# Layer 0 of a graph network: the transposed pattern made by TensorE, or from packed bytes by DMA, with the in-degrees on their own

## The chip, the cores and the metric

The kernel is one program on one core of a Trainium2 chip. The metric is the time of one execution on the device in microseconds, lower is better; times are medians of several executions. The core has a matrix engine (TensorE, PE in the profile), a vector engine (VectorE, DVE), a scalar engine (ScalarE, ACT), a general engine (GpSimd, POOL) and a sync engine (SyncE, SP). Each takes its own instructions in order; SP, ACT and POOL also issue DMA transfers.

## The reference

`x` is 2708 x 512 in float32, `adj` a symmetric 2708 x 2708 int32 matrix of zeros and ones. Four layers of a graph network run one after another, each on a normalized input, each adding its output to `x`:

```
h = relu(layernorm(x));  a = adj as float
# layer 0
x = x + relu((a.T @ h @ weight) * clip(a.sum(axis=0), 1) ** -0.5)
# layer 1: the first 64 neighbours of each row
h = relu(layernorm(x))
keep = (adj > 0) & (cumsum(adj > 0, axis=1) <= 64);  cnt = keep.sum(axis=1)
x = x + leaky(h @ W_line.T + b_line) + where(cnt > 0, leaky((keep @ h) / max(cnt, 1) @ W_nb.T + b_nb), 0)
# layer 2: attention over the neighbours, 8 heads of 64
# layer 3
h = relu(layernorm(x))
agg = (adj > 0) @ h / max(adj.sum(axis=1), 1)
x = x + relu(concat(h @ W_self + b_self, agg @ W_nb + b_nb) @ W_comb + b_comb)
```

Layer 0 multiplies with `adj` transposed, so a row block of `adj` serves as it lies, with its rows as the contracted axis. Layers 1 to 3 contract over columns and need each block of `adj` transposed.

## The kernel before

Rows are cut into `NC` = 22 chunks of `R` = 126; the last has 62 rows. `twice` and `TAIL` treat that last chunk by laying its rows down twice, at partition 0 and at 64.

**Dense parts.** Every layer has one. `staged` emits a pipeline: at step s, each stage works on chunk s minus its lag, in the order `load` (lag 0, `load_x` on SP), `normalize` (1, `norm` on VectorE with one square root on ScalarE: `ln_st` L191, `ln_mv` L193, `ln_rs`, `hn` L205), `transpose` (2, `relu_T`: `hT_ps` L214 on TensorE, evicted by ScalarE as `hT` L216) and `multiply` (3, the product). The product's result is split by `halves` into a rounded float32 and its remainder (L256, L258), two fp32r parts that later matmuls sum. There are `XBUFS` = 5 buffers for x tiles.

**Layer 0** is one long `staged` pipeline over units (g, m): six groups g of output chunks (4, 4, 4, 4, 3, 3) and, in each, all 22 row blocks m. The dense part of layer 0 is woven into group 0. A unit goes through:

- `load0`, lag 0: SP loads `ai`, the int32 block of 126 rows and up to 506 columns (5 buffers).
- `count0`, lag 4: VectorE casts it to fp32r (`ar` L450, 3 buffers), ScalarE squares it to bf16 (`ab` L452, 3 buffers), VectorE scans it (`cum` L458, 2 buffers): the running count of neighbours along the row, continued over groups through `deg` (L466).
- `sign0`, lag 5: ScalarE compares the running count with 64 (L473) and sums the signs, from which the last kept column of every row follows.
- `save0`, lag 6: stores finished rows of the residual. `multiply0`, lag 6: TensorE multiplies the block's 2 x 4 products into four accumulators (`acc` L348, through `matmuls`), then transposes the block by four matmuls with `ab` as weights and an identity (`vT_ps` L501). The identity has a column of ones, so each result carries the block's column sums too. VectorE copies these sums (L504), ScalarE evicts the transposed block as int8 into `vT` (L513), which stays in on-chip memory for layers 1 to 3.

At the last row block of a group the in-degrees are summed and turned into `nrm` (L508 to L511), the accumulators are evicted by VectorE (L531) and ScalarE (L535) by turns, and the residual x is added (L537, by GpSimd; by VectorE in the last group). `x` of a group is loaded at its middle.

The Tile framework keeps an order of instructions on each engine close to the order of emission, by its own estimates; buffers come free when their last reader is done.

**The turn to layer 1.** Three steps of layer 1's dense part are emitted within layer 0's last group, at the row blocks `AHEAD` = (9, 13, 18). The remaining ones follow: `product1` multiplies with two weights (`nb_ps`, `line_ps`, both through `product` L186), adds a bias and the leaky relu (L604, L605), and adds that to x on GpSimd (L608). `spread_last` lays the last kept columns along rows as `lastr` (L588, L594). Then layer 1's `aggregate` starts, whose weights `kt` (L623) combine `lastr` and `vT`; `vT` is read by the attention (L762) and by layer 3 (L1170) as well. In the tables below, the attention's small matmuls are at L945.

## Time and profile before

| | us |
|---|---|
| median of 3 executions | 1849.98 (1847.86 to 1853.67) |
| the profiled execution, its own time | 1852.72 |
| its span | 1850.8 |
| TensorE busy in it | 1805.7 (98%) |
| VectorE, ScalarE, GpSimd busy | 1323.8, 843.7, 211.8 |
| mean granted TensorE clock | 0.995 |

The profile is of one execution. A row of a group of instructions gives the line, engine and operation, the output and inputs with their shapes, the count, the busy time and the mean time of one in ns, then the idle time of the engine ahead of it and what ended that idle. A row of waits gives the engine and line that waited, what it waited for, the total in us, the number of times and the longest. A timeline row gives start and duration in us, and joins equal instructions (x8). Matmul durations in it overlap: the time that matters is from start to start. Layer 0 ends at about 402 us of the span, layer 1's dense part at 571.

### The profile page before, as it was taken

The numbers are of one execution on the slowest core, as the hardware profiler recorded it, in microseconds if no ns is written. First come the engines' busy times: TensorE is split into PE (matmuls) and PEld (weight loads), VectorE is DVE, ScalarE is ACT, GpSimd is POOL, SyncE is SP. The second block draws the span as 40 slices with busy tenths as digits, with TensorE's granted clock in tenths as the row PEclk, the third lists the DMA queues.
The fourth block names the chain that finished last, engine by engine and source line by source line (L and its number), as shares of the span: only waits on it lengthen the run. The fifth ranks groups of instructions, "written<-read, shape, count | busy, mean of one in ns | idle before, by whom it ended". The sixth has DMA issues, their size and how long they took to land.

```text
span 1850.8 us, 30734 instructions
## 1 busy us (share of the span) xinstructions
PE 1805.7 (98%) x11878; PEld 1050.0 (57%) x11878; DVE 1323.8 (72%) x1997; ACT 843.7 (46%) x1536; POOL 211.8 (11%) x190
## 2 busy tenths in 40 slices
PE   9999999889999999999999999999999999999998
PEld 4556667654446887754444344444344455478786
DVE  4755888874444566687889999999999777533334
ACT  2545887762220000056697776776743566500000
POOL 0001011211110112156100000000000222100000
PEclk9999999999999999999999999999999999999999
DMA  7323555542223112253330220121112444303221
GB/s 243 117 79 106 150 161 149 144 127 65 68 73 82 45 45 67 65 159 102 96 91 18 60 56 15 56 61 40 29 32 51 119 137 133 103 23 105 96 67 44
DMA packets 126027, 161.03 MB, mean 87 GB/s; under 512 B 57394, under 2 KB 77982, under 8 KB 124990
## 3 DMA queue, kind: packets, MB, share of 16 engines
q1 hardware_dynamic: 106812, 123.60, 23.1%
q10 hardware_dynamic: 18484, 33.28, 5.4%
q0 software_dynamic: 576, 2.10, 0.3%
q8 instruction: 95, 1.56, 0.3%
q14 instruction: 60, 0.49, 0.1%
HBM read 111.34 MB, written 47.42 MB: 86 GB/s over the span
## 4 chain that ended last, share of the span: by engine, by line
PE 61%; DVE 16%; issue 5%; DMA 4%; ACT 2%; POOL 0%; SPq 0%; DVEq 0%; ACTq 0%; POOLq 0%
PE acc L348 25%; PE av L945 10%; DVE t L762 9%; PE nb_ps L186 8%; PE sums L945 4%; PE wh_ps L186 4%; PE self_ps L186 4%; PE line_ps L186 4%; DVE cum L458 4%; DMA rb<-rT 2%; PE hT_ps L214 1%; DMA ai<-in_adj 1%; DMA x<-x 1%; DVE ar L450 1%; ACT cum L473 1%
## 5 line engine op out<-in xcount | busy, mean ns | idle before, releaser
L762 DVE SCALAR_TENSOR_TENSOR t<-rb,ec,vT 126x2708 f32<-126x2708 f32 (+2 forms) x220 | 532.6, 2471 | 21.5 <-PE sums L945 12.4
L348 PE MATMUL acc<-halves,kt 126*126 126x512 f32 x1848 | 434.8, 395 | 3.7 <-DVE kt L623 2.1
L945 PE MATMUL av<-t,whs 126*32 126x451 f32 (+3 forms) x4576 | 436.6, 515 | 1.3 <-ACT whs L751 0.8
L348 PEld LDWEIGHTS acc<-halves,kt 126*126 126x126 f32 x1848 | 342.6, 186 | 92.5 <-DVE kt L623 6.2
L945 PEld LDWEIGHTS av<-t,whs 126*32 126x32 f32 (+1 forms) x4576 | 161.9, 110 | 205.5 <-issue 180.1
L348 PE MATMUL acc<-halves,ar 126*126 126x512 f32 x924 | 253.2, 413 | 6.5 <-ACT vT L513 3.5
L780 ACT ACTIVATE b<-t,eb 126x2708 bf16<-126x2708 f32 (+1 forms) x78 | 199.0, 2552 | 21.6 <-DVE t L762 21.4
L348 PEld LDWEIGHTS acc<-halves,ar 126*126 126x126 f32 x924 | 163.8, 187 | 51.0 <-issue 9.2
L623 DVE SCALAR_TENSOR_TENSOR kt<-lastr,index,vT 126x504 fp32r<-126x504 int16 (+3 forms) x154 | 110.4, 728 | 81.7 <-PE acc L348 81.5
L195 ACT ACTIVATE ln_rs<-ln_mv,eps 126x1 f32<-126x1 f32 x88 | 25.6, 294 | 283.9 <-DMA x<-x 199.2
L1170 DVE CAST kt<-vT 126x504 fp32r<-126x504 int8 (+3 forms) x154 | 56.0, 366 | 137.8 <-PE acc L348 137.8
L458 DVE TENSOR_TENSOR_SCAN cum<-ai,deg 126x504 int16<-126x504 int32 (+2 forms) x110 | 126.0, 1156 | 32.9 <-DMA ai<-in_adj 21.5
L945 PE MATMUL sums<-t,whs 126*32 126x338 f32 (+5 forms) x1568 | 141.0, 451 | 5.6 <-ACT out L984 5.6
L751 ACT ACTIVATE whs<-wh,ef 126x64 f32<-126x64 f32 x220 | 76.3, 349 | 128.3 <-PE sums L945 73.1
L912 POOL TENSOR_SCALAR z<-y 126x512 f32<-126x512 f32 x22 | 44.0, 2001 | 666.9 <-DVE y L905 658.2
L473 ACT ACTIVATE cum<-cum,limit 126x504 int16<-126x504 int16 (+3 forms) x132 | 88.4, 670 | 62.1 <-DVE deg L466 60.0
L945 PEld LDWEIGHTS sums<-t,whs 126*32 126x32 f32 (+1 forms) x1568 | 56.0, 109 | 73.3 <-issue 39.1
L191 DVE BATCH_NORM_STATS2 ln_st<-x 126x6 f32<-126x512 f32 x88 | 60.4, 686 | 48.7 <-DMA x<-x 40.9
L513 ACT CAST vT<-vT_ps 126x504 int8<-126x504 f32 (+1 forms) x132 | 70.1, 536 | 29.2 <-DVE sums L504 20.0
L186 PE MATMUL nb_ps<-wfn,hT 128*126 128x512 f32 x176 | 81.2, 605 | 2.0 <-ACT hT L216 2.0
L186 PE MATMUL nb_ps<-wn,hT 128*126 128x512 f32 x176 | 81.4, 606 | 0.0
L186 PE MATMUL h_ps<-w0s,hT 128*126 128x512 f32 x176 | 79.9, 597 | 1.4 <-ACT hT L216 1.1
(178 smaller groups left out, 1972.7 us busy)
## 6 DMA issues: line engine op xcount, KB each, us to landing
x<-x SPq DMA_DIRECT2D x105, 252.0 KB
x<-x ACTq DMA_DIRECT2D x84, 252.0 KB
ai<-in_adj SPq DMA_DIRECT2D x84, 249.0 KB
x<-in_x SPq DMA_DIRECT2D x42, 252.0 KB
rb<-rT SPq DMA_DIRECT2D x7, 1332.8 KB
wh<-whd SPq DMA_DIRECT2D x70, 94.5 KB
whd<-wh SPq DMA_DIRECT2D x21, 252.0 KB
aT<-avT SPq DMA_DIRECT2D x21, 252.0 KB
```

What stands on the lines that cost most here:

```text
L186: nc.tensor.matmul(po[:n], lhsT[:, f, :n], w[:, f, :], start=(f == 0), stop=(f == NF - 1))
L191: nc.vector.bn_stats(st[:n], xc[:n])
L348: nc.tensor.matmul(acc[:R], weight[:, k * R : (k + 1) * R], parts[:, i, :], start=(m == 0 and i == 0), stop=(m == NC - 1),)
L458: nc.vector.tensor_tensor_scan(cum[:n, :gw], ai[:n, :gw], ai[:n, :gw], 0.0 if g == 0 else deg[:n, m : m + 1], op0=ALU.add, op1=ALU.max,)
L473: nc.scalar.activation(cum[:n, :gw], cum[:n, :gw], AF.Sign, bias=limit[:n], scale=-1.0, accum_out=signs[:n, m, g : g + 1],)
L513: nc.scalar.copy(vT[g][:, :, m * R : (m + 1) * R], pt[:R, :K, :R])
L623: nc.vector.scalar_tensor_tensor(by_chunk(kt, cs), lastr[:, cs[0] * R : (cs[-1] + 1) * R].rearrange("p (c r) -> p c r", r=R), index[:R, m ...
L751: nc.scalar.activation(t[:q, :O], wh.pop((u, m))[:q], AF.Copy, scale=by)
L762: ins = nc.vector.scalar_tensor_tensor(t[:q, : hi - lo], row[h][:q, lo:hi], ec[:q, m, h : h + 1], vT[g][:q, k, lo:hi], op0=ALU.max, op1=AL ...
L780: nc.scalar.activation(b[:q, : hi - lo], weight[s][:q, : hi - lo], AF.Sigmoid, bias=eb[:q, m, h : h + 1], scale=STEEP,)
L945: nc.tensor.matmul(p[j * S : (j + 1) * S, : b - a], lhsT, rhs[:, part * size + a : part * size + b], start=(s % NC == 0), stop=(s % NC == ...
L1170: nc.vector.tensor_copy(by_chunk(kt, cs), pattern(m, cs))
```

## The change

The transposed pattern is no longer made by TensorE within layer 0. Rows of `adj` and of layer 0's x are taken in pairs: of each 252 rows, the even ones form one block and the odd ones the next (`paired`). For every two blocks VectorE packs the two 0/1 values into one int16, 256 times the odd one plus the even one (`two`), and GpSimd stores it to DRAM (`packed`, 66 stores). In layer 1's dense part, each of 22 steps fetches one chunk's columns from there with two transposing DMAs issued by SP: a large one into `vT` (2-byte elements, 128 x 1264) and a small one (128 x 128) for the last rows, of which VectorE copies the part needed (`turn` at lag 4, `finish` at lag 6; the line numbers of the changed kernel are L692, L698 for the DMAs and L704 for the copy). A transposing DMA is ordered behind the load of x four chunks on. `vT` now takes the memory that layer 0's buffers leave.

The fp32r block `ar` is made by ScalarE's square, whose sum goes into a check at the end (`squares`); the bf16 block and VectorE's cast are gone. The in-degrees come from matmuls of their own: 32 columns of ones times the upper halves of `ar`, four chunks side by side in four column groups, emitted for four row blocks at a time into one accumulator; ScalarE copies that at the last but two row blocks, TensorE transposes it at the last.

`ai` has 10 buffers, `ar` 10, `cum` 5. `count0` and `sign0` of later units are ordered behind the last group's norm, evictions and copy (`fenced`), and `save0` and `multiply0` have lag 7. In the last group one residual lies in the tag "t", so that it takes no buffer of x. The row counts go to DRAM and back to be put into natural order (`degd`, `rdeg`; used at L660), ahead of x loads on SP. `lastr` is written in natural order (L675, L685).

```diff
-    ident1 = const.tile([P, P], BF16, name="ident1")
-    nc.gpsimd.memset(ident1, 1.0)
-    nc.vector.tensor_copy(ident1[:, :R], ident[:, :R])
+    oneb = const.tile([P, 32], BF16, name="oneb")
+    nc.gpsimd.memset(oneb, 1.0)
...
+    def paired(src, c):
+        if c >= NC - 2:
+            return natural(src, c)
+        first = c // 2 * 2 * R
+        return src[first : first + 2 * R, :].rearrange("(r e) d -> e r d", e=2)[c % 2]
...
-    vpool = ctx.enter_context(tc.tile_pool(name="vpool", bufs=1, side="right"))
-    vT = [vpool.tile([R, len(cs), NC * R], I8, name=f"vT{g}") for g, cs in enumerate(groups)]
+    VW = -(-NC * R // 32) * 32
+    PAIRS = -(-(NC - 2) * R // 32) * 16
+    assert NC % 2 == 0
+    vT = []
+    packed = [
+        dram.tile([NC * R // 2, len(cs) * R + P - R], I16, name=f"packed{g}")
+        for g, cs in enumerate(groups)
+    ]
+    degd = dram.tile([NC, R], F32, name="degd")
...
+                (4, lambda c: turn(c)),
+                (6, lambda c: finish(c)),
...
+                ai = wk.tile([R, WG + P - R], I32, name="ai", bufs=10)
+                block = paired(adj, m)[:, c0 : c0 + wide]
...
+            def fenced(stage):
+                def fn(i):
+                    with ExitStack() as behind:
+                        for ins in fences.values():
+                            behind.enter_context(tc.issue_after(ins))
+                        stage(i)
+                return fn
...
-                ar = wk.tile([R, WG], F32R, name="ar", bufs=3)
-                nc.vector.tensor_copy(ar[:, :gw], ai[:, :gw])
-                ab = wk.tile([R, WG + P - R], BF16, name="ab", bufs=3)
-                nc.scalar.activation(ab[:n, :wide], ai[:n, :wide], AF.Square)
-                if wide < KR + P - R:
-                    nc.gpsimd.memset(ab[:n, wide : KR + P - R], 0.0)
+                ar = wk.tile([R, WG], F32R, name="ar", bufs=10)
+                nc.scalar.activation(
+                    ar[:, :gw], ai[:, :gw], AF.Square, accum_out=squares[:R, m, g : g + 1]
+                )
                 if gw < KR:
                     nc.vector.memset(ar[:, gw:KR].bitcast(F32), 0.0)
-                cum = wk.tile([R, WG], I16, name="cum", bufs=2)
+                cum = wk.tile([R, WG], I16, name="cum", bufs=5)
...
+                if m % 2 == 0:
+                    two = wk.tile([R, WG + P - R], I16, name="two", bufs=3)
+                    nc.vector.scalar_tensor_tensor(
+                        two[:, :wide],
+                        tiles[i + 1][0][:, :wide],
+                        256.0,
+                        ai[:, :wide],
+                        op0=ALU.mult,
+                        op1=ALU.add,
+                    )
+                    if wide < KR + P - R:
+                        nc.gpsimd.memset(two[:, wide : KR + P - R], 0)
...
+                if two is not None:
+                    to = packed[g][m // 2 * R : (m // 2 + 1) * R, :]
+                    nc.gpsimd.dma_start(to, two[:, : to.shape[1]])
...
-                def products():
-                    for k, c in enumerate(cs):
-                        matmuls(acc[c], h0[m], ar, k, m)
-                if m < NC - 1:
-                    products()
-                pt = ps.tile([P, KMAX, P], F32, name="vT_ps", tag="ps")
-                for k in range(K):
-                    nc.tensor.matmul(
-                        pt[:, k, :], ab[:n, k * R : k * R + P], ident1[:n], start=True, stop=True
+                uppers[m] = ar.bitcast(BF16)
+                batch = range(0)
+                if m == NC - 3:
+                    for j in (1, 2):
+                        uppers[m + j] = tiles[i + j][0].bitcast(BF16)
+                    batch = range(m // 4 * 4, NC)
+                elif m % 4 == 3:
+                    batch = range(m - 3, m + 1)
+                if m == 3:
+                    sums[g] = ps.tile([P, 2 * P], F32, name="sums_ps", tag="ps")
+                for j in batch:
+                    q = rows(j)
+                    for k in range(K):
+                        nc.tensor.matmul(
+                            sums[g][k * 32 : (k + 1) * 32, :R],
+                            oneb[:q],
+                            uppers[j][:q, 2 * k * R + 1 : 2 * (k + 1) * R : 2],
+                            start=(j == 0),
+                            stop=(j == NC - 1),
+                        )
+                if m == NC - 3:
+                    by_col = sums[g, 0] = common.tile([P, D], F32, name="by_col", tag="t", bufs=3)[:, :R]
+                    ins = nc.scalar.copy(by_col[: K * 32], sums[g][: K * 32, :R])
+                    fences["act"] = ins.ins
+                for k, c in enumerate(cs):
+                    matmuls(acc[c], h0[m], ar, k, m)
+                if m == NC - 1:
+                    pt = sums.pop(g)[:R, P:]
+                    nc.tensor.transpose(
+                        pt[:, : K * 32], sums.pop((g, 0))[: K * 32], ident[: K * 32, : K * 32]
                     )
-                nc.vector.tensor_copy(sums[g][:, :K, m : m + 1], pt[:R, :K, R : R + 1])
-                if m == NC - 1:
-                    nrm = small.tile([R, KMAX], F32, name="nrm")
-                    total = ind[:R, cs[0] : cs[-1] + 1]
-                    nc.vector.tensor_reduce(total, sums[g][:, :K], AX.X, ALU.add)
-                    nc.vector.tensor_scalar(nrm[:, :K], total, 1.0, None, op0=ALU.max)
+                    nrm = sums[g, 1] = small.tile([R, KMAX, 1], F32, name="nrm")
+                    nc.vector.tensor_scalar(
+                        nrm[:, :K],
+                        pt[:, : K * 32].rearrange("p (k j) -> p k j", j=32)[:, :, :1],
+                        1.0,
+                        None,
+                        op0=ALU.max,
+                    )
                     nc.scalar.activation(nrm[:, :K], nrm[:, :K], AF.Sqrt)
-                    nc.vector.reciprocal(nrm[:, :K], nrm[:, :K])
-                    products()
-                nc.scalar.copy(vT[g][:, :, m * R : (m + 1) * R], pt[:R, :K, :R])
+                    ins = nc.vector.reciprocal(nrm[:, :K], nrm[:, :K])
+                    fences["dve"] = ins.ins
...
+                    for k, c in enumerate(cs):
+                        tag, bufs = ("t", 3) if g == len(groups) - 1 and k == 0 else ("x", XBUFS)
+                        xs[c] = load_x(x_in, c, tag=tag, bufs=bufs)
...
+                        fences["dve"] = ins.ins
                     else:
-                        nc.scalar.activation(r[:n], po[:n], AF.Relu, scale=nrm[:n, k : k + 1])
+                        ins = nc.scalar.activation(r[:n], po[:n], AF.Relu, scale=nrm[:n, k])
+                        fences["act"] = ins.ins
...
+                (4, fenced(count0)),
+                (5, fenced(sign0)),
+                (7, save0),
+                (7, multiply0),
...
+        vpool = ctx.enter_context(tc.tile_pool(name="vpool", bufs=1))
+        vT.extend(
+            vpool.tile([P, len(cs), VW], mybir.dt.uint8, name=f"vT{g}")
+            for g, cs in enumerate(groups)
+        )
...
+        even = NC - 2
+        nc.sync.dma_start(
+            degd[:even].rearrange("(b f) r -> b (f r)", f=2).rearrange("b (r e) -> r b e", e=2),
+            deg[:R, :even].rearrange("r (b e) -> r b e", e=2),
+        )
+        nc.sync.dma_start(degd[even:].rearrange("c r -> r c"), deg[:R, even:])
         rdeg = const.tile([P, NC], F32, name="rdeg")
-        nc.vector.tensor_scalar(rdeg, deg, 1.0, None, op0=ALU.max)
+        nc.gpsimd.memset(rdeg, 1.0)
+        nc.sync.dma_start(rdeg[:R], degd.rearrange("c r -> r c"))
+        rcnt = const.tile([P, NC], F32, name="rcnt")
+        nc.vector.tensor_scalar(rcnt, rdeg, float(NEIGHBORS), 1.0, op0=ALU.min, op1=ALU.max)
...
+        def turn(c):
+            g, k = where[c]
+            own = slice(k * R, k * R + P)
+            with tc.issue_after(loads[min(c + 4, NC - 1)]):
+                nc.sync.dma_start(
+                    vT[g][:, k, : 2 * PAIRS].bitcast(I16), packed[g][:PAIRS, own], transpose=True
+                )
+            ends = wk.tile([P, P], I16, name="ends", bufs=4)
+            with tc.issue_after(loads[min(c + 4, NC - 1)]):
+                nc.sync.dma_start(ends, packed[g][NC * R // 2 - P :, own], transpose=True)
+            turned[c] = ends
+        def finish(c):
+            g, k = where[c]
+            ends = turned.pop(c)
+            nc.vector.tensor_copy(
+                vT[g][:, k, (NC - 2) * R : NC * R].rearrange("p (e r) -> p e r", e=2),
+                ends[:, P - R :].bitcast(mybir.dt.uint8).rearrange("p (r e) -> p e r", e=2),
+            )
+            nc.vector.memset(vT[g][:, k, N:], 1)
+            if c == NC - 1:
+                move(nc.sync, vT[g][TAIL : TAIL + last_rows, k, :], vT[g][:last_rows, k, :])
```

## The prediction

> **What bounds the kernel now.** I read the page first, then the busy time by stretch, then the timeline of TensorE inside a group, the table of waits, the chain where layer 0 ends, and one step of layer 1's dense part.
>
> ```profile
> span 1850.8 us, 30734 instructions
> PE 1805.7 (98%) x11878; PEld 1050.0 (57%) x11878; DVE 1323.8 (72%) x1997; ACT 843.7 (46%) x1536; POOL 211.8 (11%) x190
> L348 PE MATMUL acc<-halves,ar 126*126 126x512 f32 x924 | 253.2, 413 | 6.5 <-ACT vT L513 3.5
> ```
>
> TensorE is busy 98% of the span, so only work taken from it, or idle taken from it, counts. The stretches below are groups 0 (from its middle), 1, 3, 4 and 5 of layer 0, the turn to layer 1, and layer 1's dense part (span, then busy time and count per engine, granted clock, DMA share, GB/s).
>
> ```profile
> 62.00:178.50 116.50, 113.68 (x461) 67.10 (x460) 67.87 (x161) 62.08 (x141) 1.36 (x3) 1.00 0.29 87
> 178.50:229.10 50.60, 47.76 (x261) 34.41 (x261) 41.44 (x94) 40.28 (x92) 7.19 (x6) 1.00 0.54 156
> 278.80:328.00 49.20, 47.84 (x268) 35.22 (x268) 41.82 (x94) 40.07 (x94) 8.56 (x8) 1.00 0.49 144
> 328.00:369.00 41.00, 37.53 (x205) 26.59 (x204) 34.92 (x101) 32.05 (x91) 6.95 (x10) 1.00 0.53 153
> 369.00:401.00 32.00, 31.53 (x178) 22.57 (x177) 27.19 (x105) 26.02 (x79) 6.74 (x23) 1.00 0.39 115
> 401.00:413.60 12.60, 8.22 (x24) 4.04 (x23) 6.77 (x15) 2.90 (x6) 0.07 (x1) 0.90 0.54 168
> 413.60:570.60 157.00, 157.00 (x435) 73.59 (x435) 69.23 (x139) 31.67 (x64) 27.82 (x22) 0.99 0.23 72
> ```
>
> Groups 1 to 5 last 222.5 us with 212.5 busy (group 2 is 49.7 with 47.8): 10.0 us idle. The dense part has none: what is added there to other engines is free until it makes TensorE wait.
>
> ```profile
> 254.24 0.40 PE L501 MATMUL vT_ps<-ident,ab 126*128 126x128 bf16 x4
> 254.45 2.10 PE L348 MATMUL acc<-halves,ar 126*126 126x512 f32 x8
> 256.39 0.40 PE L501 MATMUL vT_ps<-ident,ab 126*128 126x128 bf16 x4
> 1044.32 0.47 PE L945 MATMUL sums<-b,parts 126*32 126x338 bf16 x8
> 1044.61 1.70 PE L945 MATMUL av<-t,whs 126*32 126x451 f32 x16
> ```
>
> A unit of four chunks repeats every 2.15 us. Layer 1 runs 814 of the same products in 188.72 us without a gap, 0.232 each; eight are 1.855, so the four transposes cost 0.30, 75 ns each. The last two lines are from the attention: eight 32-column matmuls of 338 columns take 0.29 us from start to start, 36 ns each.
>
> ```profile
> ACT cum L473 <- DVE deg L466: 24.6, 28, 1.5
> DVE cum L458 <- DMA ai<-in_adj: 21.5, 18, 3.1
> DVE cum L458 <- ACT cum L473: 10.3, 22, 1.6
> ```
>
> VectorE and ScalarE wait on each other's few buffers and on the integer loads. The last chain is the end of layer 0:
>
> ```profile
> 403.17 4.31 DMA x<-x
> 407.57 3.42 DMA x<-x
> 412.50 1.07 PE hT_ps L214 x4
> ```
>
> A residual is stored, its buffer is loaded with layer 1's x, and only then can TensorE go on: 4.38 us idle, and the next eight `nb_ps` take 5.87 us instead of 3.60 at a granted clock of 0.90. That is 6.65 us lost.
>
> **Removed from TensorE.** 22 row blocks by 22 chunks are 484 transposes (L501): 484 x 0.075 = -36.3 us. With them go the int8 evictions on ScalarE (0.571), the bf16 copy there (0.621), the fp32r cast on VectorE (0.467) and the copy of the sums (0.157).
>
> **Added to TensorE.** 484 matmuls of 126 columns against 32 ones, in batches of sixteen over four column groups. Nearest row: 36 ns at 338 columns. If columns set it, 126 would take less; if a fixed cost sets it, the same. The Trainium skill ("TensorE: Matmul & The Clock Gate", Part 1, on the step from 56 to 53.3 ns) states a floor of about 25 ns start to start however small the matmul. By that floor the sum is 12.1 us, by the row 16.9. These read every second bf16 element, which the row doesn't, so I take 35 ns: +16.9. Bounds: 9.7 (20 ns) and 36.3 (75 ns, the row of the transposes). Six transposes of the sums are below 1 us. Net -19.4.
>
> **VectorE and ScalarE in layer 0.** VectorE per unit before: cast 0.467, scan 1.295, count 0.147, sums 0.157, together 2.07 against TensorE's 2.15: 0.09 spare, so that a 3 us stall takes over 30 units to repay. After: scan and count, plus half of one packing operation (nearest: a 512-element operation of two inputs, 0.69, so 0.34): 1.79, against a new TensorE period of 2.15 - 0.30 + 0.14 = 1.99: 0.20 spare. ScalarE: square 0.62 with its accumulator read 0.19, sign 0.71: 1.52, where it had 1.90. TensorE stays the bound. `ai` goes from 5 buffers to 10, `ar` from 3 to 10, `cum` from 2 to 5, which is what the three waits hang on, and the fences put the norm and evictions of a group ahead of later steps. What is queued behind them: scans and squares of later units, which then have up to a few units of stock. I take 9 of the 10.0 us of idle as removed. Bounds: 13 (the ends of matmuls are modelled, so some idle may hide in busy time) and 0. At the start no stock exists and counting now runs ahead of the normalizing of x, which TensorE waits for: 0 to +4, I take +1.
>
> **Queues in layer 0.** GpSimd gets 66 stores of packed bytes. Its own DMA issues took 0.72 and 0.89 us: some 53 us in 375, beside about 8 of 50 busy per group. An addition of x (1.57 us) may stand 0.9 behind one; nobody waits for it but SP's stores. Traffic grows by 126 KB per two units, 30 GB/s on 156: hidden as long as loads run ten units ahead.
>
> **The turn to layer 1.** One residual of the last group lies in another tag, so three x tiles of layer 1 can be loaded before the end. I take 5 of 6.65 us as gained. Against it: two stores of degrees and a load of them, 4-byte elements, go ahead of the next x loads on SP, and in VectorE's order the use of the loaded degrees (L660) stands before the last group's norm, its evictions and the next `hn`. Nearest rows: 4.31 us for a store and 3.42 for a load, 7.7 in series, from the last count, which runs three units (some 4.5 us) before the last products: 3 us late, partly beside 7 us of matmuls of chunk 0. 0 to +4, I take +1.5.
>
> **The transposes in the dense part.** Each of 22 steps puts two transposing DMAs on SP behind the x load of chunk c+4, 323 and 32 KB, and the copy of the last columns (L704) on VectorE behind that load's statistics. So behind a late transpose stand the rest of that norm, the next `hn`, the evictions (L722 and L266 of the changed kernel), and on SP the next x load. One step of before:
>
> ```profile
> 446.12 0.69 DVE L191 BATCH_NORM_STATS2 ln_st<-x 126x6 f32<-126x512 f32 x1 [2.71 <-DMA x<-x]
> 447.32 0.54 DVE L205 TENSOR_SCALAR hn<-x,ln_mv,ln_rs 126x512 f32<-126x512 f32 x1
> 452.58 0.59 PE L214 MATMUL hT_ps<-ident,hn 126*128 126x126 f32 x4
> ```
>
> The norm waited for the load, issued 443.4 and landed 446.1 (2.7 us), and `hn` was ready 4.7 us before TensorE took it. The period is 7.3 us, so a load and a pair of transposes fit if the pair takes under 7.3 - 2.7 = 4.6. No row of before shows such a DMA. The skill speaks both ways. "VectorE: DVE Perf Modes" ("The three transpose paths") gives 1309 ns for one 128x128 by DMA against 390 on TensorE, and prefers TensorE: the pair holds 1392/128 = 10.9 such blocks, 14.2 us if they go one after another, or 22 x (14.2 + 2.7 - 7.3) = +211 us. "DMA: Bandwidth & Descriptors" ("Latency and other measured facts") gives 261 GB/s: 356 KB in 1.4 us, +0. I take the second, with a fixed part, some 3 us: in this trace 252 KB of plain load landed in 2.7 us, most of it fixed, so a block's 1.3 us alone should be mostly fixed too. Cost 0. L704 and its memset are some 0.5 us per step (an estimate from the casts' 0.467) beside VectorE's 69 of 157 us. If the cover is gone, each us above 4.6 costs 22.
>
> **Sum.** -19.4 - 9 + 1 - 5 + 1.5 = -30.9 on the profiled execution's 1852.72 (span 1850.8), 1822 there. That execution is 2.7 above the median, so 1849.98 - 30.9 = 1819.
>
> **Rivals.** (1) Slow transposes, the other side: one mechanism, the pair above 4.6 us. The gain of 31 is used up at 4.6 + 31/22 = 6.0 us. At 8 us it is 22 x 3.4 - 31 = +44, 1894; at 14.2, 2030. For it: the 1309 ns and no row here; against: 72 GB/s of traffic in that part and the bandwidth above. (2) Half the gain: the small matmuls cost 60 to 75 ns because of their strided reading, or the pair takes about 5 us (+9): -31 + 12 to 19, 1831 to 1838. For it: the stride; against: the 36 ns row. (3) All of it: 25 ns, all 10 us of idle, 6.65 at the turn: -24.2 - 10 - 6.65, 1809, and 1804 with the idle at 13 and nothing spent elsewhere.
>
> **Numbers.** 0.3% is 5.5 us, about what a measurement of this kernel can tell from no change. Forecast as summed (1812 to 1828): 0.45. All of it, down to 1800: 0.15. Half the gain, up to 1844: 0.19. About nothing (1844 to 1855.5): 0.04. Slow transposes, slower: 0.17. So faster 0.79, same 0.04, slower 0.17. The range leaves out what is under 1800 and most of the slow case: 1800 to 1857.
>
> **What would show it.** Right: no L501; groups 1 to 3 at 43 to 44 us each instead of 50; batches of sixteen small matmuls in about 0.56 us; an idle under 2 us before the second chunk's `hT_ps`; the dense part still 157 us, with pairs landing within 4 us of issue and L704 waiting little. Wrong: a dense part well over 160 us with L704 waiting for transposes; small matmuls above 60 ns; groups still near 48, with VectorE waiting for loads or for stores to free `two`; last norms waiting for the degrees.

## The result, and the profile after

The changed kernel takes 1825.11 us at the median (1822.74 to 1831.35), the one before 1851.33 in the same comparison: a ratio of 0.9865, with a 95% interval from 0.9835 to 0.9895. The forecast was 1819, with 1812 to 1828 as its middle range. The profiled execution of the changed kernel has a span of 1823.8 us where before had 1850.8, 27.0 less; the forecast had 30.9.

The page of the changed kernel:

```profile
span 1823.8 us, 30715 instructions
PE 1785.4 (98%) x11884; PEld 1041.1 (57%) x11884; DVE 1308.3 (72%) x1836; ACT 796.6 (44%) x1542; POOL 245.2 (13%) x241
L368 PE MATMUL acc<-halves,ar 126*126 126x512 f32 x924 | 235.4, 408 | 4.3 <-ACT ar L488 2.4
```

Groups 1, 4 and 5 from last product to last product, first before the change and then after it (span, then busy time and count of TensorE, its weight loads, VectorE, ScalarE and GpSimd, granted clock, DMA share, GB/s). The prediction's stretches of before were cut up to 5.3 us behind the last products, so its idle times differ a little from these.

```profile
174.90:223.80 48.90, 47.01 (x262) 34.31 (x260) 40.53 (x94) 38.48 (x88) 7.19 (x6) 1.00 0.51 149
322.90:364.00 41.10, 36.37 (x197) 25.53 (x196) 34.28 (x94) 31.55 (x88) 7.09 (x9) 1.00 0.51 147
364.00:400.80 36.80, 36.23 (x201) 25.83 (x201) 32.04 (x123) 30.97 (x93) 8.10 (x24) 1.00 0.40 116
```

```profile
175.40:218.40 43.00, 43.00 (x264) 33.10 (x263) 38.98 (x58) 31.85 (x92) 13.23 (x16) 1.00 0.69 200
304.30:342.10 37.80, 35.39 (x198) 25.64 (x197) 31.80 (x65) 27.01 (x93) 13.05 (x19) 0.95 0.60 180
342.10:380.20 38.10, 35.37 (x202) 26.61 (x201) 27.48 (x79) 23.07 (x85) 11.58 (x22) 0.96 0.42 113
```

In the groups of four chunks TensorE has no idle left: 43.0 us each where it was 49 to 50. In the groups of three there is idle, 2.4 and 2.7 us, together as much as before (4.7 and 0.6), and the granted clock is 0.95 and 0.96 where it was 1.00. So these two took almost as long as before the change.

The table gives every kernel's time with the ratio to the kernel before, and stages of its profile. A group runs from the start of the first product with the last row block (`acc<-tail,ar`) in the group before it to the same product of its own; "turn and dense" runs from that product of the last group to the first one of layer 1's aggregate. The kernel before was measured anew with each set of runs.

| kernel | median us | ratio, 95% interval | groups 1, 2, 3 | 4 + 5 | turn and dense |
|---|---|---|---|---|---|
| before | 1850.06 to 1851.77 | 1 | 48.9, 50.0, 49.2 | 78.1 | 170.5 |
| changed | 1825.11 | 0.9865 [0.9835, 0.9895] | 42.9, 43.0, 43.0 | 76.2 | 165.5 |
| `e1_two8` | 1820.95 | 0.9847 [0.9823, 0.9871] | 42.9, 43.0, 43.0 | 70.1 | 165.0 |
| `e2_add_dve` | 1821.35 | 0.9842 [0.9818, 0.9865] | 42.9, 43.0, 43.0 | 69.2 | 168.9 |
| `e3_deg_late` | 1820.55 | 0.9846 [0.9821, 0.9871] | 42.9, 43.0, 43.0 | 73.2 | 163.3 |
| `e12_both` | 1818.32 | 0.9830 [0.9815, 0.9846] | 42.9, 43.0, 43.0 | 70.4 | 163.3 |
| `e4_few_bufs` | 1850.68 | 0.9998 [0.9988, 1.0008] | 49.5, 49.6, 48.4 | 77.7 | 167.9 |
| `e6_ar6` | 1839.33 | 0.9946 [0.9930, 0.9963] | 47.8, 48.9, 47.7 | 74.7 | 165.1 |
| `e7_ai7_cum2` | 1848.96 | 0.9987 [0.9974, 1.0001] | 47.5, 48.5, 49.0 | 77.6 | 169.7 |
| `e11_cum2` | 1849.64 | 0.9993 [0.9985, 1.0002] | 50.5, 50.8, 49.1 | 77.1 | 167.8 |
| `e9_no_fence` | 1864.14 | 1.0069 [1.0048, 1.0090] | 43.8, 59.3, 58.0 | 83.9 | 163.3 |
| `e5_before_stock` | 1879.98 | 1.0167 [1.0140, 1.0195] | 51.1, 56.9, 57.2 | 82.7 | 171.4 |
| `e10_before_stock_fence` | 1859.98 | 1.0043 [1.0025, 1.0062] | 48.3, 50.4, 50.1 | 76.7 | 173.1 |
| `e8_turn_twice` | 1843.50 | 0.9957 [0.9947, 0.9967] | 42.9, 43.0, 43.0 | 74.0 | 174.1 |

What lies behind layer 1's dense part takes 1280.4 us in the profile of before and 1278.8 after. In the others it is between 1275.7 and 1281.8, except for `e8_turn_twice` with 1291.9. Differences of two or three us between single profiles are thus no evidence by themselves. Nor do the times of the runs tell `e1_two8`, `e2_add_dve` and `e3_deg_late` from the changed kernel: their intervals overlap with its own. What counts below is an idle stretch of TensorE that comes or goes at a named place.

### The profile page after: what moved, and what is told of

Read it like the earlier page. It is cut to its first block, busy times and chain, and to the rows that moved or that the text cites. A ratio compares the mean times of both kernels' runs of the same rounds, so it can differ in the third digit from the quotient of the medians.

```text
span 1823.8 us, 30715 instructions
## 1 busy us (share of the span) xinstructions
PE 1785.4 (98%) x11884; PEld 1041.1 (57%) x11884; DVE 1308.3 (72%) x1836; ACT 796.6 (44%) x1542; POOL 245.2 (13%) x241
## 4 chain that ended last, share of the span: by engine, by line
PE 77%; DVE 11%; DMA 5%; issue 4%; POOL 1%; ACT 1%; SPq 0%; ACTq 0%; DVEq 0%; POOLq 0%
PE acc L368 32%; PE av L1066 16%; PE nb_ps L184 6%; PE sums L1066 6%; DVE t L883 5%; PE self_ps L184 4%; PE wh_ps L184 3%; PE line_ps L184 2%; PE h_ps L184 2%; DVE cum L494 2%; PE fused_ps L312 2%; PE hT_ps L212 1%; DMA x<-x 1%; DMA rb<-rT 1%; DMA packed<-two 1%
## 5 line engine op out<-in xcount | busy, mean ns | idle before, releaser
L368 PE MATMUL acc<-halves,ar 126*126 126x512 f32 x924 | 235.4, 408 | 4.3 <-ACT ar L488 2.4
L368 PEld LDWEIGHTS acc<-halves,ar 126*126 126x126 f32 x924 | 171.0, 189 | 55.4 <-issue 8.1
L1291 DVE CAST kt<-vT 126x504 fp32r<-126x504 uint8 (+3 forms) x154 | 55.9, 365 | 138.2 <-PE acc L368 138.2
L184 PE MATMUL wh_ps<-w2s,hT 128*126 128x512 f32 (+1 forms) x176 | 79.4, 593 | 0.0
```

Of the source, the lines that this page charges most:

```text
L184: nc.tensor.matmul(po[:n], lhsT[:, f, :n], w[:, f, :], start=(f == 0), stop=(f == NF - 1))
L368: nc.tensor.matmul(acc[:R], weight[:, k * R : (k + 1) * R], parts[:, i, :], start=(m == 0 and i == 0), stop=(m == NC - 1),)
L1291: nc.vector.tensor_copy(by_chunk(kt, cs), pattern(m, cs))
```

## Experiments on groups 4 and 5: the step that failed

In the changed kernel the chain of waits through group 4 has this part:

```profile
320.22 5.52 DMA packed<-two
325.76 0.55 DVE two L506
326.32 0.93 DVE cum L494
328.22 0.51 ACT ar L488 x2
328.77 2.92 PE acc L368 x6
```

The packing on VectorE has three buffers. At 325.76 it has waited for the store that frees one, and behind it in VectorE's order stand the scans, and behind these ScalarE's squares that TensorE needs. In the whole group VectorE waits 3.7 us for such stores (1.33, 1.97 and 0.39 us); in group 5 it waits 2.2.

Theory A of the two experiments below takes these stores to be late because GpSimd adds the residuals first. GpSimd's own timeline speaks against that:

```profile
306.06 6.31 POOL L613 TENSOR_TENSOR x<-x,y 126x512 f32<-126x512 f32 x4 [6.92 <-issue]
313.08 0.53 POOL L539 DMA_DIRECT2D packed<-two  x1 [0.71 <-DVE deg L502]
315.46 0.53 POOL L539 DMA_DIRECT2D packed<-two  x1 [1.85 <-DVE deg L502]
```

GpSimd is idle before each store and waits for VectorE, and each store of group 4 goes out 0.3 us after its packing has ended. What is long is the way to DRAM: the five stores issued between 312 and 323 us took 4.5 to 6.9 us to land, those between 324 and 341 us 2.3 to 3.1. In the first stretch (312 to 326 us) the DMA engines move 252 GB/s, in the second (327 to 341 us) 166; whether that is the reason was not tested. The additions hold VectorE in other ways, shown below.

**More buffers for the packed tile.**

```diff
-                    two = wk.tile([R, WG + P - R], I16, name="two", bufs=3)
+                    two = wk.tile([R, WG + P - R], I16, name="two", bufs=8)
```

> The packed tile gets 8 buffers instead of 3; nothing else. In the changed kernel groups 4 and 5 last 38.0 and 37.9 us from first to last product, where 22 units of three chunks need some 32.5 each. Theory A (stores of packed bytes stand behind GpSimd's additions of x, the three buffers stay full, and VectorE stops at the packing, with the scans behind it): groups 4 and 5 together shorten by 7 to 10 us, the waits of the packing on its store go to near 0, the time to about 1816. Theory B (VectorE has no time to spare in units of three chunks, 1.45 to 1.50 us against TensorE's 1.47, so any stall stays): 0 to 2 us. Theory C (GpSimd's additions stretch VectorE's scans while both run): 0 to 2 us, with scans of 1.6 us as before.

Groups 4 and 5 in its profile (columns as above), and below them the same of `e3_deg_late`, which keeps the three buffers:

```profile
304.60:340.60 36.00, 34.35 (x201) 25.48 (x200) 31.79 (x67) 27.29 (x94) 13.08 (x19) 1.00 0.64 191
340.60:374.60 34.00, 33.13 (x201) 25.18 (x200) 27.22 (x78) 22.94 (x84) 11.33 (x22) 1.00 0.44 125
```

```profile
305.20:342.40 37.20, 34.05 (x197) 24.89 (x196) 31.16 (x61) 26.31 (x91) 13.07 (x19) 1.00 0.62 183
342.40:378.20 35.80, 33.84 (x201) 25.45 (x200) 28.11 (x84) 23.78 (x89) 11.59 (x22) 1.00 0.44 123
```

With eight buffers they are 6.1 us shorter than in the changed kernel, a little under theory A's 7 to 10, and the packing no longer waits for a store. So these waits were on TensorE's path. Theory B falls: VectorE had the time. Nearly all of the 6.1 us lies in two parts. Idle falls from 5.1 to 2.5 us, and the products take 3.3 us less because the clock is back at 1.00. Only the first part is steady: with three buffers, `e3_deg_late` has 5.1 us of idle and `e8_turn_twice` 4.5, but the clock stays at 1.00 in the first, so that its groups take 73.2 us. The repair is thus worth 3 to 6 us, by whether the clock falls with the idle.

**The additions on VectorE.**

```diff
-                    eng = nc.gpsimd if g < len(groups) - 1 else nc.vector
+                    eng = nc.gpsimd if g < len(groups) - 3 else nc.vector
```

> The residual additions of groups 3 and 4 go from GpSimd to VectorE (7 additions of some 0.69 us); groups 0 to 2 keep theirs on GpSimd. Theory A: the stores are no longer behind additions of 1.6 us each, groups 4 and 5 shorten by 4 to 6 us. Theory C: the same, and scans next to group ends fall from 1.6 to 1.0 us. Theory B: VectorE has 4.8 us more to do in the two groups where it is the bound, so they lengthen by 3 to 5 us.

7.0 us shorter, with 1.9 us of idle. But the packing still waits 2.7 us for stores in group 4, and these again go out 0.3 us after the packing. So the edit helps in another way than theory A's. The turn and dense part came out 3.4 us longer in this profile: TensorE waits for `hn` there for 2.71 us where the changed kernel waits 1.43, and 1.01 us for an earlier chunk.

The same stretch bears on theory C. In the changed kernel, VectorE right after group 3 (start, duration; the additions on GpSimd ran from 306.06 to 312.37):

```profile
308.06 3.24 DVE L494 TENSOR_TENSOR_SCAN cum<-ai,deg 126x378 int16<-126x378 int32 x2
311.27 1.52 DVE L506 SCALAR_TENSOR_TENSOR two<-ai 126x380 int16<-126x380 int32 x1
314.63 0.53 DVE L506 SCALAR_TENSOR_TENSOR two<-ai 126x380 int16<-126x380 int32 x1
```

With the additions on VectorE (`e2_add_dve`) the same operations, and one of the waits that remain, are:

```profile
312.71 1.00 DVE L494 TENSOR_TENSOR_SCAN cum<-ai,deg 126x378 int16<-126x378 int32 x1
313.63 0.53 DVE L506 SCALAR_TENSOR_TENSOR two<-ai 126x380 int16<-126x380 int32 x1
326.50 0.56 DVE L506 SCALAR_TENSOR_TENSOR two<-ai 126x380 int16<-126x380 int32 x1 [2.25 <-DMA packed<-two]
```

A scan takes 1.6 us instead of 1.0 and a packing 1.5 instead of 0.5 while GpSimd adds: 2.2 us in two scans and one packing. VectorE also waits 1.5 us for the additions with an eviction (`y` L605). Against these 3.7 us stand the four additions, 2.6 us on VectorE; its first packing ends 7.1 us behind the last product of group 3, in the changed kernel 8.4.

So two delays of VectorE meet in group 4, the additions on GpSimd and the landing of the stores. `e1_two8` takes away the second alone and `e2_add_dve` mainly the first, and either is enough: TensorE's stock covers one of them and not both. Theory A named the buffers rightly and the queue wrongly; theory C's stretching is one part of the cause.

**The degrees used later.** The reciprocals and limits made from the reloaded degrees (L660 and the three lines after it) go into a function that is emitted at chunk 6 of the dense part, behind that chunk's `y`:

```diff
         def save_last(c):
+            if c == 6:
+                with tc.issue_after(h1["y"]):
+                    counts()
```

> The use of the reloaded degrees (reciprocals and limits) is moved from ahead of the last group's norm to the middle of layer 1's dense part on VectorE; stores and load stay. The 12.2 us wait of VectorE for the load of the degrees goes. Theory that the wait is on the path: TensorE's 1.43 us idle before the third hT_ps goes too and the time falls by 1.5 to 3 us. Theory that chunks 0 and 1 cover it, as in the changed kernel where TensorE ran two chunks (14.6 us) meanwhile: within 1.5 us of the changed kernel.

In the changed kernel the wait was there:

```profile
DVE rcnt L660 <- DMA rdeg<-degd: 12.2, 1, 12.2
DVE vT L704 <- DMA ends<-packed: 23.5, 12, 3.0
DVE two L506 <- DMA packed<-two: 10.8, 9, 2.2
```

and the chain of waits at the turn shows what it waited for, and the one place where TensorE paid (timeline):

```profile
371.35 10.00 DMA degd<-deg
381.40 3.38 DMA rdeg<-degd
```

```profile
396.89 0.65 PE L212 MATMUL hT_ps<-ident,hn 126*128 126x126 f32 x4 [1.43 <-DVE hn L203]
```

With the late use the wait and that idle are gone, and turn and dense part take 163.3 us instead of 165.5. The first theory held for this stage (2.2 us, of which 1.4 are that idle). The rest of the lower profile, 3 us in groups 4 and 5, is not the edit's: the idle there is the same (5.1 us) and the clock is not, as shown above.

**Both repairs.**

> The two repairs together: 8 buffers for the packed tile, and the degrees used in the middle of the dense part. Alone they ended layer 1's dense part 6.3 and 4.0 us earlier than the changed kernel in their profiles, in different stages: groups 4 and 5, and the turn with the steps behind it. If they add up, the dense part ends some 8 to 10 us earlier and the time is about 1815; if the second only covers what the first leaves, 1819 to 1821.

1818.32 us: from the end of group 0 to layer 1's aggregate 362.6 us, against 370.5 in the changed kernel and 363.9 and 365.4 with one repair. That is 8.0 us in the profile, and 6.8 at the median of the runs, between the two outcomes set down beforehand. It is the fastest of these kernels, though its interval meets those of the single repairs.

## Experiments on buffers and order: what the gain rests on

**Fewer buffers.** First all three, then one part at a time.

```diff
-                ai = wk.tile([R, WG + P - R], I32, name="ai", bufs=10)
+                ai = wk.tile([R, WG + P - R], I32, name="ai", bufs=7)
-                ar = wk.tile([R, WG], F32R, name="ar", bufs=10)
+                ar = wk.tile([R, WG], F32R, name="ar", bufs=6)
-                cum = wk.tile([R, WG], I16, name="cum", bufs=5)
+                cum = wk.tile([R, WG], I16, name="cum", bufs=2)
```

> Fewer buffers: ai 7 instead of 10, ar 6 instead of 10, cum 2 instead of 5; all else as changed. If the stock of units is what removes the idle in groups 1 to 3 (6.1 us beside TensorE's busy time before, 0 after), 4 to 10 us come back over groups 1 to 5. If the shorter work of VectorE and ScalarE per unit is enough by itself, groups 1 to 3 stay at 43.0 us each and the time within 2 us of the changed kernel.

The whole gain is gone, with the same work on TensorE as in the changed kernel: the 484 transposes are still out. `e6_ar6` takes only the middle edit, `e7_ai7_cum2` the first and the last, `e11_cum2` only the last:

> Only the multiplied block ar has fewer buffers, 6 instead of 10. With the few buffers of the earlier run (ai 7, ar 6, cum 2) groups 1 to 3 lasted 49.5, 49.6 and 48.4 us instead of 43.0. The batch of small matmuls reads four blocks at once, so up to four are held until it ran. Theory that ar alone sets the stock: 48 to 50 us per group again and about 1848. Theory that the scan's buffers or the loads do: 43 to 44 us and about 1826.

> The other half of the same run: ai 7 instead of 10 and cum 2 instead of 5, ar stays at 10. If ar alone sets the stock, groups 1 to 3 stay at 43.0 us and the time at 1825 within 4 us; if the scan (two buffers between VectorE and ScalarE) or the loads set it, 46 to 50 us per group and up to 1848.

> Only the scan's buffers go back from 5 to 2. With ai 7 and cum 2 groups 1 to 3 lasted 47.5, 48.5 and 49.0 us. If the two buffers that VectorE's scan and ScalarE's comparison pass between them set this, about 48 us per group and 1845 or more; if the loads with 7 buffers do, 43 to 44 us and 1825 within 4.

Fewer buffers for the scan alone, or for `ar` alone, bring the groups back to 47.5 to 51 us; fewer for `ai` alone was not tried. So no one of them sets the stock by itself. Groups 1 and 2 with two scan buffers, and below them group 1 of the changed kernel:

```profile
177.10:227.60 50.50, 46.44 (x263) 35.39 (x262) 39.23 (x58) 31.52 (x91) 13.22 (x16) 0.93 0.61 174
227.60:278.40 50.80, 46.63 (x262) 35.00 (x261) 41.05 (x61) 32.58 (x94) 13.21 (x16) 0.93 0.65 187
```

```profile
174.40:217.30 42.90, 42.90 (x262) 33.02 (x261) 37.88 (x58) 30.98 (x90) 13.23 (x16) 1.00 0.69 199
```

TensorE does the same 262 or so matmuls. Of the 7.6 us that group 1 is longer, 4.1 are idle and 3.5 are matmuls at a lower clock (0.93). The idle comes in two waits (timeline of TensorE with `e11_cum2`), and the chain of waits behind them is of the kind seen in groups 4 and 5:

```profile
195.98 7.39 PE L368 MATMUL acc<-halves,ar 126*126 126x512 f32 x24 [1.84 <-ACT ar L488]
205.89 0.24 PE L557 MATMUL sums_ps<-ar,oneb 126*32 126x126 bf16 x4 [2.22 <-ACT ar L488]
206.06 9.25 PE L368 MATMUL acc<-halves,ar 126*126 126x512 f32 x32
215.58 7.70 PE L368 MATMUL acc<-halves,ar 126*126 126x512 f32 x32
```

```profile
187.47 6.18 DMA packed<-two
193.67 0.07 DVE two L506
195.09 1.19 DVE cum L494
196.35 5.81 DMA ai<-in_adj
202.28 0.69 DVE two L506
202.97 1.19 DVE cum L494
```

A store takes 6.18 us to land; until then VectorE stands at the packing (2.7 us), and ScalarE's square, which TensorE needs, waits for VectorE. Only the scan that follows frees a buffer of `ai`, so the next load goes out at 196.35, and its landing makes VectorE wait a second time (3.8 us). In `e6_ar6` the chain to the idle of group 1 goes through a store of 5.0 us. In the changed kernel VectorE waits for stores too, five times in groups 1 to 3 and 4.9 us in all, but TensorE lives through it on its stock of units. So what the stock covers here is in good part a delay that the change brought itself. Whether two scan buffers would do with eight packed tiles was not run.

After the second wait 32 products take 9.25 us, and 7.70 ten us later: the idle is paid once as idle and once more as clock. One limit of these four runs: the framework also orders instructions by the buffers it has (with two scan buffers VectorE's and SP's order differs in places), so a buffer count and the order that comes with it are not told apart.

**Without the ordering.**

```diff
-                        for ins in fences.values():
-                            behind.enter_context(tc.issue_after(ins))
```

> The changed kernel without the ordering of count0 and sign0 behind each group's norm, evictions and copy; buffers as changed. If the ordering is what keeps group ends short, groups 1 to 3 go from 43.0 us to 45 to 50 and the time to 1835 to 1850; if the stock alone does it, they stay at 43 to 44 and the time within 4 us of 1825.

39 us slower than the changed kernel, and slower than the kernel before. Two lines of the table of waits and one of the timeline say where (line numbers are two lower in this kernel):

```profile
DVE cum L492 <- DMA ai<-in_adj: 42.7, 10, 5.5
PE sums_ps L570 <- ACT by_col L564: 17.1, 2, 9.2
```

```profile
230.20 0.48 PE L570 MATMUL sums_ps<-ident,by_col 128*126 128x128 f32 x1 [9.20 <-ACT by_col L564]
```

Squares and comparisons of the next group, which themselves wait for scans and those for loads, stand on ScalarE ahead of the 0.24 us copy of the in-degrees; TensorE waits 9.2 us for that copy at the end of one group.

**Buffers and ordering without the change of work.** The kernel before, its evictions going to a scratch tile so that the memory is free (layers 1 to 3 then read ones, so only layer 0 is compared), `vT` allocated behind layer 0, and ai, ar, ab and cum with 10, 8, 8 and 5 buffers; then the same with fences on `nrm` and the evictions and lag 7 (a part of the edit):

```diff
-    vT = [vpool.tile([R, len(cs), NC * R], I8, name=f"vT{g}") for g, cs in enumerate(groups)]
+    vT = []
-                nc.scalar.copy(vT[g][:, :, m * R : (m + 1) * R], pt[:R, :K, :R])
+                scratch = wk.tile([R, KMAX, R], I8, name="scratch", bufs=3)
+                nc.scalar.copy(scratch[:, :K], pt[:R, :K, :R])
```

> The kernel before with its transposes kept, but with layer 0's memory freed as the change frees it: the evicted pattern goes to a rotating scratch tile, vT is allocated after layer 0 and filled with ones by GpSimd in layer 1's dense part (so layers 1 to 3 work on another pattern), and ai, ar, ab and cum have 10, 8, 8 and 5 buffers. Theory that the stock of units is what removes the idle: groups 1 to 3 fall from 48.9, 50.0 and 49.2 us (last product to last product) to the 47.4 us that 22 units of 2.155 need, groups 4 and 5 from 78.2 to about 73. Theory that VectorE, with 0.09 us to spare per unit, can't fill the stock: they stay within 0.5 us of before.

> As the earlier run of the kernel before with freed memory and more buffers (layers 1 to 3 work on another pattern, filled with ones), and now with count0 and sign0 ordered behind each group's norm and evictions and with lag 7 for multiply0. Without the ordering groups 1 to 3 lasted 51.1, 56.9 and 57.2 us. If stock and ordering together remove the idle whatever TensorE has to do, they fall to 47.4 to 48.0 us; if VectorE's and ScalarE's work with the transposes in TensorE is too long for that (0.09 us to spare), they stay at 49 or more.

Without the ordering the groups grow to 57 us, with it they are 48.3, 50.4 and 50.1, no better than before. So room and order gain nothing while the work stays, as taking the work away gained nothing with a short stock or without the order. In group 2 of `e10_before_stock_fence` TensorE idles 3.0 us, and each wait ends with ScalarE: evictions of the transposed block (0.88 and 0.76 us), squares `ab` (0.26 and 0.72) and an eviction `y` (0.36). The change takes the evictions of the block off ScalarE and the cast off VectorE. What holds ScalarE there was not followed further.

## Experiment on the transposing DMAs

```diff
             with tc.issue_after(loads[min(c + 4, NC - 1)]):
                 nc.sync.dma_start(
                     vT[g][:, k, : 2 * PAIRS].bitcast(I16), packed[g][:PAIRS, own], transpose=True
                 )
+            with tc.issue_after(loads[min(c + 4, NC - 1)]):
+                nc.sync.dma_start(
+                    vT[g][:, k, : 2 * PAIRS].bitcast(I16), packed[g][:PAIRS, own], transpose=True
+                )
```

> The large transposing DMA of each step is issued twice, 44 instead of 22, into the same place. In the changed kernel a pair was issued at 399.44 us and the copy L704 that waits for it ran at 404.88, 5.4 us, and the dense part kept its 157.4 us. Theory of the forecast (load and pair one after another within a step of 7.3 us): a load of 2.7 and then about 8 us are over the step by 3.4, so the dense part lengthens by 22 x 3.4 = 75 us. Theory that load and transposes overlap on the DMA engines and only the landing of the last one counts: about 8 us from the load's issue are over the step by less than 1 us, some 0 to 20 us.

In the changed kernel SP's timeline shows a step like this:

```profile
399.07 0.33 SPq L101 DMA_DIRECT2D x<-x  x1
399.44 1.26 SPq L692 DMA_TRANSPOSE vT<-packed  x1
400.75 1.23 SPq L698 DMA_TRANSPOSE ends<-packed  x1
```

and VectorE's, in the same step:

```profile
401.84 0.69 DVE L189 BATCH_NORM_STATS2 ln_st<-x 126x6 f32<-126x512 f32 x1 [0.87 <-DMA x<-x]
404.88 0.29 DVE L704 COPY vT<-ends 128x252 uint8<-128x252 uint8 x1 [2.35 <-DMA ends<-packed]
```

The load lands 2.7 us after its issue, the pair 5.4 us after its own (the copy runs 4.2 to 6.2 us after it over the 22 steps), side by side and not one after the other, and the next `hT_ps` still finds its `hn` ready. The second large one writes the same place, so it goes out only when the first has landed, and lands some 3.4 us after its own issue (414.17 to 417.59 us in one step). From the first issue to the copy it is 7.2 to 7.7 us in most steps, and VectorE waits nearly every time:

```profile
DVE vT L708 <- DMA vT<-packed: 60.3, 21, 6.7
```

Turn and dense part take 8.6 us more, and what follows 13.1 us more (1291.9 against 1278.8): the last transposes come up to 12 us after issue, and layer 1's aggregate begins by waiting for them. Together 22 us in the profile and 18 at the medians, near the upper end of the second theory and far from the 75 of the first. So the forecast's limit of 4.6 us for the pair was wrong: at more than 7 us from first issue to copy the stage lost 8.6 us, and not 22 times the excess.

## Why the prediction was right, and where it was not

Added up by place, in us of the profiled executions. The forecast's terms are split here by where they lie: 0.040 us for each of 88 blocks in a group of four and 66 in a group of three, the idle by the prediction's stretches of before (6.1 in groups 1 to 3; of the 3.9 in groups 4 and 5, 2.9), and the terms of the start and the turn.

| place | forecast | measured |
|---|---|---|
| to the end of group 0 | -2.5 | +0.7 |
| groups 1 to 3 | -16.7 | -19.2 |
| groups 4 and 5 | -8.2 | -1.9 |
| turn and dense part | -3.5 | -5.0 |
| behind it | 0 | -1.6 |
| sum | -30.9 | -27.0 |

The mechanism was right where most of the gain lies, in groups 1 to 3. That the sum came so near is in part luck: small matmuls that cost 5.2 us less than forecast stand against 6.3 us missing in groups 4 and 5.

- **TensorE's transposes.** That they were worth 36.3 us of its time can't be seen alone, but nothing in the groups of four contradicts it: 22 units of 1.855 us of products and 88 small matmuls (1.97 us) make 42.8 of the 43.0 us, with no idle.
- **The small matmuls.** The term was mis-sized, in favour: 16 take 0.35 us (below, start to start), 22 ns each, and 12 in three column groups 0.34, 28 ns each. So here the time followed the number in one column group, about 0.09 us for each set side by side. All 484 cost 11.7 us (four groups of four batches of 16 and one of 24, 1.97 us each, and two groups of 1.93), not 16.9. The floor of 25 ns that the Trainium skill states ("TensorE: Matmul & The Clock Gate", Part 1) did not bind the batches of sixteen; the measurement decides.

```profile
224.06 0.42 PE L557 MATMUL sums_ps<-ar,oneb 126*32 126x126 bf16 x16
224.41 2.81 PE L368 MATMUL acc<-halves,ar 126*126 126x512 f32 x11
```

- **The idle of groups 1 to 3** went from 6.1 us to nothing, as forecast, and the stock and the order are needed for it: `e4`, `e6`, `e7` and `e11` bring idle back by buffers, `e9` by the order. But the forecast treated this as a gain of 9 us beside 19 of work. With the work gone and two scan buffers, the kernel is as slow as before, by 4.1 us of idle and 3.5 of lower clock in a group. In the chains of `e11` and `e6` the late stores of the next point stand behind that idle: the stock had to cover a delay that the change made and the forecast did not have.
- **The step that failed** is the one on GpSimd's queue, "nobody waits for it but SP's stores", by which stores of packed bytes and additions cost nothing. VectorE waits for both: in group 4 3.7 us at the packing, for stores through three buffers, and 1.5 us for an addition, and its own operations take 2.2 us longer while GpSimd adds. The forecast named stores that free `two` too late among its signs of being wrong, but its sum had nothing for them. Groups 4 and 5 came out 6.3 us longer than forecast in the profile of the changed kernel (3.3 in that of `e3`, where the clock held); `e1` and `e2`, with 70.1 and 69.2 us, meet the forecast's 69.9.
- **The degrees.** The queue was named rightly and its price was wrong: 7.7 us from the rows for full rows of x, 13.4 measured (10.00 and 3.38 in the chain), most of it for the stores, which go in 4-byte elements. The cover was wrong too, 7 us of one chunk where TensorE had chunks 0 and 1 (14.6 us of matmuls). The two errors cancel: 1.4 us of idle were left, and the term of +1.5 was right by luck.
- **The transposes** cost TensorE next to nothing, as forecast, on a wrong limit: they overlap with the load. A pair took 4.2 to 6.2 us from issue to copy, between the forecast's 1.4 us by bandwidth and 14.2 by blocks, and above the 4 us that it named as a sign of being right. VectorE did wait for them, twelve times and 23.5 us in all, but behind the turn TensorE idles only once in the dense part, 0.35 us for `hn`. Each takes 1.2 to 1.4 us of SP's time to issue in most steps, which the forecast did not count.
- **Group 0** came out 3.2 us worse than forecast. The loss lies between 62 and 100 us, where TensorE idles 4.8 us (before 1.5), once 2.6 us for `hT`, at a clock of 0.96 (before 1.00), while VectorE is busy 34.5 of the 38 us (before 25.7). This fits the forecast's fear that counting runs ahead of normalizing, mis-sized at +1, but no run tested it. Kernels with the same code in group 0 (`e2`, `e3`, `e8`) end it 1.2 to 2.7 us later still.

## What to carry to other kernels

Moving work off the bounding engine pays only if the engines ahead of it keep a stock: here the same removal was worth 26 us with ten, ten and five buffers and the group's end ordered ahead of later work, and nothing with two scan buffers. Ask then which delay the stock has to cover, and whether the change itself made it. When work is put on an idle engine, look at who waits for its end, and count the buffers against the time to landing and not to issue: three packed tiles, with stores that landed after 5.5 to 6.9 us, cost 3 to 6 us. When two repairs each give back nearly the whole loss, look for two delays of which the stock can cover one. A delay of fixed length that long periods absorb shows first where the period is short, here in the groups of three chunks.

## What the runs showed of the hardware

- A wait of about two us on TensorE can be paid twice: after one of 2.22 us (`e11_cum2`) 32 products took 9.25 us at a granted clock of 0.82, and 7.70 later at 1.00. Shorter waits, of 1.07 and 1.10 us in groups 4 and 5 of `e3_deg_late`, left the clock at 1.00.
- Two of VectorE's operations took 1.6 and 2.9 times as long while GpSimd ran its two-input additions (scan 1.6 instead of 1.0 us, packing 1.52 instead of 0.53).
- A transposing DMA of 323 KB and one of 32 KB take nearly the same time to issue on SP, 1.26 and 1.23 us, against 0.31 to 0.33 for a plain load. Pairs back to back at the end of the dense part went out every 2.7 us.
- Equal stores from GpSimd (about 93 KB) took 4.5 to 6.9 us to land when issued between 312 and 323 us of the changed kernel, and 2.3 to 3.1 between 324 and 341.
- Of two stores of degrees, 11 KB in 4-byte elements, the second, issued 1.9 us behind the first, landed 10.0 us after its issue; loads of 252 KB in full rows landed after 2.7 to 2.8.
